# Deformable convolution on one core: tiles of 36 output bases whose samples for all nine taps come from one product, instead of patches of 128 source pixels scattered into the output

## The chip, the core and the metric

The kernel runs on one core of a Trainium2 chip. The metric is the device time of one execution in microseconds (us), from launch to the last output; the figures below are a median of three runs and one execution taken by the hardware profiler. All arithmetic is in 32-bit floats.

## The reference

The input x holds 8 images of 128 channels, 64 x 64 pixels. Two layers follow one another, each added to its own input.

Layer 0 normalises the channels in 32 groups, then does a modulated deformable convolution with 3 x 3 taps, then a batch normalisation over all images and a ReLU:

```python
om = lax.conv_general_dilated(x, off_w, (1, 1), ((1, 1), (1, 1)), ...)
off = om[:, :2 * KK].reshape(B_, KK, 2, H_, W_)
mask = jax.nn.sigmoid(om[:, 2 * KK:])
...
py = off[:, :, 0] + (row - 1.0) + ky
px = off[:, :, 1] + (column - 1.0) + kx
y0, x0 = jnp.floor(py), jnp.floor(px)
ly, lx = py - y0, px - x0
...
val = (corner(y0, x0, (1 - ly) * (1 - lx)) + corner(y0, x0 + 1, (1 - ly) * lx)
       + corner(y0 + 1, x0, ly * (1 - lx)) + corner(y0 + 1, x0 + 1, ly * lx))
val = val * mask[:, None]
out = jnp.einsum('bckhw,ock->bohw', val, w.reshape(w.shape[0], C, KK))
```

For every output pixel and each of nine taps, a learned offset (two numbers) and a mask (one) come from an ordinary 3 x 3 convolution with 27 outputs. The tap reads the image bilinearly at its shifted place, zero outside, times the mask. The nine samples are then mixed over channels by the tap's 128 x 128 weights and summed.

Layer 1 normalises in groups again and is a mixture of experts: four 3 x 3 convolutions weighted by a gate of each image, with the best two kept, and a shared one.

## The kernel before

The kernel has two ways for layer 0. `dense()` is the one that runs here: it holds for offsets under 2 in size (`REACH = 2`), which it counts as it goes; `general()` follows only where an offset is larger. The bilinear weight of a source pixel for a tap is a product of two tents, one in y and one in x: relu(1 - |distance|). For a given tap only the 5 x 5 source pixels around the tap's own place can have a weight that is not zero.

**Tables.** For each image `tables(b)` loads the image into `pad`, normalises it in place (L305-306), runs the offset convolution on TensorE (L335), writes offsets and masks to DRAM and reads them back with rows, and columns, on partitions (L351-371). Then, for each of the five distances, ScalarE computes the tents and VectorE multiplies the y tent by the mask (L386-402), and the results go to two tables in DRAM, `y_table` (SP's queue, L406) and `x_table` (POOL's queue, L416). The tables have rows of zeros at the rim. They are written one image ahead: `tables` is a generator that the main loop advances by a step here and there (`made`), so that its instructions lie between those of the loop.

**Patches.** The work is done from the side of the source. A patch is 8 rows x 16 columns of source pixels (`PR`, `PC`), the 128 of them on partitions: 256 patches for 8 images. Three steps are done for each patch and each tap row ky:

- `z_part` (L469, L475): the patch's pixels times the tap weights of three taps, a product with 384 columns; ScalarE copies it from PSUM (`pz`) to SBUF (`z`). The source pixels have been put in the patch's order before by `repack` (L240).
- `weights` (L487): VectorE multiplies the y weights (`ywts`) by the x weights (`xwts`) to get `s`: for each source pixel, three taps and each of up to 12 x 20 outputs around the patch, the bilinear weight.
- `s_part` (L508): for each tap a product of `z` (source pixel by output channel) with `s` (source pixel by output place), added in PSUM into `py`, shifted by the tap's place. Products of 18 taps, of two patches one above the other, are summed there.

`collect` (L525) then adds `py` to the half image `y` on VectorE. `end_half` takes the statistics for the batch normalisation and stores `y` to DRAM (`yd`, L546-547).

The weights of a source pixel stand at a place in the partition's row that depends on its own place in the patch, so the tables are loaded in strips: `load_tx` (POOL's queue, L437) copies one source column's x weights to the 8 partitions of that column, 16 DMAs for a block of four patches; `load_ty` (SP's queue, L451) copies one source row's y weights to 16 partitions, 8 DMAs for two patches. Places outside the strips hold zeros for good (L222).

Each engine works through its instructions in the program's order (`manual_schedule`). In the main loop the weights of the next patch come ahead of the sampling of this one:

```python
for ky in range(3):
    weights(i + 1, ky)
    s_part(i, ky, py)
    z_part(i + 1, ky)
    next(made, None)
```

A DMA waits in its queue, SP's or POOL's, until what it reads is written and the buffer that it fills is free, and those behind it wait with it.

**Layer 1** (from L820 on) reads `yd` back, applies batch normalisation and ReLU, adds the input, and does the mixture of experts as one mixed 3 x 3 convolution (L1050) for each image.

Of the kernel before, what the change touches and what calls it, by code (L numbers as in the profile page):

```python
# [16 lines left out]
P = 128  # L17
# [22 lines left out]

REACH = 2
NR = 2 * REACH + 1
PR, PC = 8, 16
NRB, NCB = H // PR, W // PC
WR, WC = PR + 2 * REACH, PC + 2 * REACH
UR, UC = WR + 2, WC + 2
ROWPAD = REACH + 1
NQI = H + 2 * ROWPAD
GSTEP = TAPS * WC
GROW = NR * GSTEP  # L50
CARRY = 24
LATER = 4
HROWS = H // 2 + 2 * ROWPAD
HSTEP = TAPS * HROWS
# [4 lines left out]
def deform_moe_conv(  # L59
# [46 lines left out]
    ystats = const.tile([P, B * NCH, 6], F32, name="ystats")  # L106
# [37 lines left out]
    def padded(pool, name):  # L144
# [9 lines left out]


    n_y, n_x = NCB * NQI * GROW, 2 * NQI * NR * HSTEP
    fill = -(-max(n_y, n_x) // (P * 256))
    tables_of = [[dram.tile([P * fill * 256], F32, name=f"tab{a}{i}") for i in range(2)] for a in "yx"]
    y_table = [
        tables_of[0][b % 2][:n_y].rearrange("(c q n) -> c q n", c=NCB, q=NQI) for b in range(B)  # L160
    ]
    x_table = [
        tables_of[1][b % 2][:n_x].rearrange("(h q n) -> h q n", h=2, q=NQI) for b in range(B)
    ]
# [11 lines left out]
    def row_range(r, ky):  # L176
        return max(0, 1 + ky - PR * r), min(WR, H - PR * r + 1 + ky)

    def col_range(c, kx):
        return max(0, 1 + kx - PC * c), min(WC, W - PC * c + 1 + kx)  # L180

    def windows(t, ky):

        one = t[:, 3 * ky : 3 * ky + 1, 2 : 2 + WC]
        return bass.AP(
            tensor=one.tensor, offset=one.offset,
            ap=[list(one.ap[0]), [PC, NCB], [WP6 - 1, 3], [1, WC]],
        )

    def dense():  # L190

        with ExitStack() as st:
# [4 lines left out]
            ap4 = st.enter_context(tc.tile_pool(name="d4", bufs=5))  # L197
            ps_c = st.enter_context(tc.tile_pool(name="ps_c", bufs=2, space=PSUM))
            ps_z = st.enter_context(tc.tile_pool(name="ps_z", bufs=3, space=PSUM))
            ps_y = st.enter_context(tc.tile_pool(name="ps_y", bufs=2, space=PSUM))  # L200

            zeros = a1.tile([P, 256], F32, name="zeros")
# [14 lines left out]


            x_wts = [a1.tile([P, WC, 3, 3, HROWS], F32, name=f"xwts{i}") for i in range(2)]
            y_wts = [a1.tile([P, 2, WR, TAPS, WC], F32, name=f"ywts{i}") for i in range(3)]  # L220
            for t in (x_wts[0], y_wts[0], y_wts[1], x_wts[1], y_wts[2]):
                nc.gpsimd.memset(t, 0.0)  # L222
# [6 lines left out]
            dw_sb = a1.tile([P, TAPS * P], F32, name="dw_sb")  # L229
            xh, ys, ss, zs = {}, {}, {}, {}  # L230
            blocks = [(b, h, c) for b in range(B) for h in range(2) for c in range(NCB)]
            patches = [(t, r) for t in range(len(blocks)) for r in range(NRB // 2)]
            per_image = len(patches) // B

            def repack(b, h):

                xh[b, h] = a2.tile([P, NRB // 2, NCB, PC, PR], F32, name="xh")
                for r in range(NRB // 2):
                    r0 = 1 + PR * (h * NRB // 2 + r)
                    nc.scalar.copy(  # L240
                        xh[b, h][:, r].rearrange("p c x y -> p y c x"),
                        pad[:, r0 : r0 + PR].rearrange("p y (c x) -> p y c x", c=NCB),
                    )
                    yield

            def tables(b):
# [8 lines left out]
                if b:  # L255
                    yield from repack(b - 1, 1)
                if b == B:
                    return
                for q in range(4):
# [5 lines left out]
                    yield  # L265
                if b < 2:
                    for t in tables_of:
                        nc.sync.dma_start(
                            out=t[b].rearrange("(p a n) -> p a n", p=P, n=256),
                            in_=zeros.unsqueeze(1).to_broadcast([P, fill, 256]),  # L270
                        )
# [842 lines left out]
```

## Time and profile before

| | |
|---|---|
| time, median of 3 runs | 2019.41 us (2015.37 to 2022.78) |
| the profiled execution's own time | 2019.38 us |
| its span | 2017.7 us |
| first sampling product (L508) | 100.7 us |
| last sampling product ends | 1631.2 us |
| layer 1 starts to load (L866) | 1640.3 us |
| TensorE busy, of the span | 1860.5 us, 92% |
| VectorE busy | 1647.3 us, 82% |
| ScalarE busy | 724.4 us, 36% |
| GpSimd (POOL) busy | 698.9 us, 35% |
| moved by DMA | 290.28 MB, mean 144 GB/s |
| mean granted clock of TensorE | 0.973 |

The profile gives, for each group of instructions, source line, engine, operation, the tiles written and read, the shapes, the count, then the busy time in us and the mean of one in ns, then the idle time of the engine just ahead of them and what ended it. PE is TensorE's matmuls, PEld its loads of weights, DVE VectorE, ACT ScalarE, POOL GpSimd; SPq is the queue of SyncE. A window gives the busy time of each engine in a stretch of the span. Every 32-bit matmul appears as two records. Times are of one execution, so durations are read from one and the same run.

### The profile page before, as it was taken

Reading aid. Unit: us, or ns where it says so; the run is one execution under the profiler, and the core shown is the slowest. Engines: PE = TensorE matmul, PEld = TensorE weight load, DVE = VectorE, ACT = ScalarE, POOL = GpSimd, SP = SyncE. Lnnn points to the kernel's source line nnn. Section 1 sums busy time; section 2 is a strip of 40 time slices with the busy share of each in tenths; the row PEclk is TensorE's granted clock in tenths of the full one; section 3 lists DMA queues with packets and bytes.
Section 4 is the critical chain, followed back from the end, with each engine's and each line's share of the span. In section 5 each row is a group of like instructions: output and inputs, shape, how many; then the busy total and the mean of one; then the engine's idle time right before and its main releaser. Section 6 shows DMA issues by size and latency. Waiting matters only on the chain. (4 is left out here: it accounts for less than half of the span.)

```text
span 2017.7 us, 25073 instructions
## 1 busy us (share of the span) xinstructions
PE 1860.5 (92%) x8146; PEld 1304.4 (65%) x8146; DVE 1647.3 (82%) x1760; ACT 724.4 (36%) x1266; POOL 698.9 (35%) x1225
## 2 busy tenths in 40 slices
PE   4099999999999999999999999999999937999999
PEld 1086787678767876786677667767888833444443
DVE  1196899599969996997799779969999959888883
ACT  1332443244324432443353234334433223333420
POOL 5323453243334342443153325333443323232220
PEclk9599999999999999999999999999999978999999
DMA  3584776477648764785478557856776554443311
GB/s 100 112 209 88 167 165 169 88 176 158 167 93 183 185 140 96 171 199 122 116 161 196 106 122 162 195 109 141 158 159 145 109 190 168 181 173 136 136 42 63
DMA packets 187755, 290.28 MB, mean 144 GB/s; under 512 B 113792, under 2 KB 119168, under 8 KB 187616
## 3 DMA queue, kind: packets, MB, share of 16 engines
q1 hardware_dynamic: 151008, 225.44, 43.6%
q0 software_dynamic: 36608, 63.14, 14.6%
q8 instruction: 68, 1.11, 0.3%
q14 instruction: 71, 0.58, 0.1%
HBM read 231.54 MB, written 56.84 MB: 143 GB/s over the span
## 5 line engine op out<-in xcount | busy, mean ns | idle before, releaser
L487 DVE TENSOR_TENSOR s<-xwts,ywts 128x684 f32<-128x684 f32 (+6 forms) x768 | 1159.4, 1564 | 80.4 <-DMA xwts<-tabx 49.8
L508 PEld LDWEIGHTS py<-s,z 128*128 128x128 f32 x4608 | 836.7, 190 | 304.4 <-issue 89.1
L508 PE MATMUL py<-s,z 128*128 128x240 f32 (+10 forms) x4608 | 993.1, 352 | 40.8 <-DVE s L487 27.2
L437 POOL DMA_DIRECT2D xwts<-tabx x1024 | 512.4, 505 | 744.1 <-DVE s L487 531.7
L475 ACT COPY z<-pz 128x384 f32<-128x384 f32 x768 | 368.8, 481 | 937.2 <-PE pz L469 936.5
L469 PE MATMUL pz<-dw_sb,xh 128*128 128x384 f32 x1536 | 624.1, 488 | 28.5 <-ACT xh L240 28.5
L469 PEld LDWEIGHTS pz<-dw_sb,xh 128*128 128x128 f32 x1536 | 285.5, 191 | 38.8 <-ACT xh L240 29.4
L1050 PE MATMUL pc<-v,u 128*128 128x512 f32 x384 | 172.5, 599 | 13.2 <-DVE v L1000 13.2
L1050 PE MATMUL pc<-v,wmix 128*128 128x512 f32 x384 | 173.5, 597 | 0.0
L897 POOL TENSOR_TENSOR x<-x,xt 128x512 f32<-128x512 f32 x64 | 90.8, 1446 | 162.8 <-ACT x L896 158.4
L335 PE MATMUL pc<-pad,offw_sb 128*32 128x504 f32 (+1 forms) x1152 | 135.1, 593 | 7.9 <-ACT pad L306 7.9
L1050 PEld LDWEIGHTS pc<-v,u 128*128 128x128 f32 x384 | 72.6, 191 | 102.8 <-issue 86.6
L1050 PEld LDWEIGHTS pc<-v,wmix 128*128 128x128 f32 x384 | 71.3, 189 | 87.0 <-issue 84.1
L525 DVE TENSOR_TENSOR y<-py,y 128x418 f32<-128x418 f32 (+2 forms) x128 | 75.7, 592 | 62.0 <-PE py L508 61.9
L416 POOL DMA_DIRECT2D tabx<-work x80 | 52.0, 653 | 205.1 <-ACT work L390 193.9
L335 PEld LDWEIGHTS pc<-pad,offw_sb 128*32 128x32 f32 x1152 | 33.4, 109 | 94.0 <-issue 81.5
L1026 ACT ACTIVATE t<-pc,bmix 128x512 f32<-128x512 f32 x32 | 22.0, 687 | 186.5 <-PE pc L1050 104.8
L318 DVE TENSOR_SCALAR om<-pc,offb_sb 128x512 f32<-128x512 f32 x16 | 12.0, 751 | 80.0 <-ACT om L315 80.0
L399 DVE TENSOR_TENSOR work<-work,mask 64x240 f32<-64x240 f32 x120 | 41.6, 403 | 36.2 <-ACT work L388 36.2
L240 ACT COPY xh<-pad 128x512 f32<-128x512 f32 x64 | 71.0, 1141 | 0.2
L930 ACT ACTIVATE pad<-x,shift,scale 128x512 f32<-128x512 f32 x64 | 47.5, 805 | 47.8 <-DVE shift L923 35.3
L896 ACT ACTIVATE x<-x,yshift,yscale 128x512 f32<-128x512 f32 x64 | 46.9, 803 | 19.9 <-DMA x<-yd 19.9
(109 smaller groups left out, 705.3 us busy)
## 6 DMA issues: line engine op xcount, KB each, us to landing
ywts<-taby SPq DMA_DIRECT2D x1024, 112.5 KB
xwts<-tabx POOLq DMA_DIRECT2D x1024, 53.4 KB, 5.8
pad<-in_x_dram SPq DMA_DIRECT2D x32, 512.0 KB
yd<-y SPq DMA_DIRECT2D x64, 256.0 KB
x<-yd SPq DMA_DIRECT2D x32, 512.0 KB
xt<-in_x_dram SPq DMA_DIRECT2D x32, 512.0 KB
out_dram<-yo SPq DMA_DIRECT2D x32, 512.0 KB
taby<-work SPq DMA_DIRECT2D x120, 60.0 KB
```

What stands on the lines that cost most here:

```text
L240: nc.scalar.copy(xh[b, h][:, r].rearrange("p c x y -> p y c x"), pad[:, r0 : r0 + PR].rearrange("p y (c x) -> p y c x", c=NCB),)
L335: nc.tensor.matmul(pc[32 * j : 32 * j + 32].rearrange("p (h w) -> p h w", w=W)[:, :, lo:hi], lhsT=offw_sb[:, k, :], rhs=pad[:, r : r + 8, ...
L416: nc.gpsimd.dma_start(out=bass.AP(tensor=x_table[b].tensor, offset=x_table[b].offset + first, ap=[[NR * HSTEP, W], [NR * HSTEP + 3 * HROWS ...
L437: nc.gpsimd.dma_start(out=flat[qx * PR : (qx + 1) * PR, qx * HSTEP : (qx + NR) * HSTEP], in_=src.unsqueeze(0).to_broadcast([PR, NR * HSTEP]),)
L469: nc.tensor.matmul(pz, lhsT=xh[b, h][:, r, c].rearrange("p x y -> p (x y)"), rhs=dw_sb[:, 3 * ky * P : 3 * (ky + 1) * P], start=True, stop ...
L475: nc.scalar.copy(zs[i][:, 3 * ky * P : 3 * (ky + 1) * P], pz)
L487: nc.vector.tensor_tensor(s[:, :, lo:hi, cl:ch], x_wts[t % 2][:, cl:ch, :, ky, first + lo : first + hi].rearrange("p c k r -> p k r c"), y ...
L508: nc.tensor.matmul(py[:, top + lo : top + hi, cl - kx + 2 : ch - kx + 2], lhsT=zs[i][:, k * P : (k + 1) * P], rhs=s[:, kx, lo:hi, cl:ch], ...
L525: nc.vector.tensor_tensor(part, py[:, rl:rh, cl:ch], part, ALU.add)
L897: nc.gpsimd.tensor_tensor(y, y, xt[:, c * CH : (c + 1) * CH], ALU.add)
L930: nc.scalar.activation(pad2[:, 1 + 8 * c : 9 + 8 * c, 1 : W + 1], x1[:, c * CH : (c + 1) * CH].rearrange("p (h w) -> p h w", w=W), AF.Iden ...
L1050: nc.tensor.matmul(pc, lhsT=us[j][:, kx], rhs=vs[g][:, rows, kx : kx + W], start=(kx == 0), stop=(kx == 2),)
```

## The change

Layer 0's `dense()` is turned round: the work is done from the side of the output, and the tap weights come last.

- **Tiles and bands.** The output has 66 x 66 bases with its rim, cut in 11 x 11 tiles of 6 x 6 = 36 (`T`). A base stands for the place to which a tap at its own offset 0 points, so the sample of tap (ky, kx) at output (r, c) belongs to base (r + ky, c + kx). The samples of a tile need 10 x 10 = 100 source pixels (`Q`, `QQ`). A band is one row of 11 tiles; there are 88 bands and 968 tiles.
- **Source pixels on partitions.** After normalising, `tables` transposes the image on TensorE (32 transposes of 128 x 128), ScalarE copies them out of PSUM, and two DMAs for each group of four write them to `pixels` in DRAM, pixel by pixel with 128 channels. Ten DMAs from DRAM to DRAM rearrange these as `tiled`, so that one DMA for each band (`xts`) brings, for every tile, its 100 pixels onto 100 partitions.
- **Weights.** One VectorE product for each tile makes `s`: for each of 100 source pixels the weights of all nine taps at 36 bases, 324 elements. The y and x weights come by 10 DMAs each for every band (`load`), on SP's and POOL's queues, with 10 equal copies each; three buffers of each.
- **Sampling.** One product for each tile (`sample`), 100 x 128 by 100 x 324, gives all taps' samples in channel order; ScalarE copies them to `samples`, a strip of 8 rows x 66 columns for each tap. Its first two rows are copied from the band before.
- **Tap weights.** Nine products for each band (`conv`), 128 x 128 by up to 384 columns, sum the taps in PSUM, one band behind the sampling. `finish` adds the bias on ScalarE, takes the statistics and stores.
- **Out go** `z_part`, `s_part`, `collect`, `start_half`, `end_half`, `repack`, `load_tx`, `load_ty`. The table writes change in form: y weights with 3 DMAs for each distance in runs of 66 elements, x weights with 3 in runs of 18. The advance of `tables` in the loop is 14 steps a band. The offset convolution, the tents and layer 1 stay as they are; `bn_aggr` moves from layer 1's head to the end of layer 0.

The diff, cut to its core:

```diff
-PR, PC = 8, 16
...
+T = 6
+Q = T + 2 * REACH
+QQ = Q * Q
+NT1 = (H + 2) // T
+WB = W + 2
...
+    pixels = dram.tile([H, NQI, P], F32, name="pixels")
+    tiled_of = [dram.tile([NQI, Q, NT1, P], F32, name=f"tiled{i}") for i in range(2)]
...
-            x_wts = [a1.tile([P, WC, 3, 3, HROWS], F32, name=f"xwts{i}") for i in range(2)]
-            y_wts = [a1.tile([P, 2, WR, TAPS, WC], F32, name=f"ywts{i}") for i in range(3)]
...
+            x_wts = [a1.tile([P, NT1, T, TAPS, T], F32, name=f"xwts{i}") for i in range(3)]
+            y_wts = [a1.tile([P, T, TAPS, WB], F32, name=f"ywts{i}") for i in range(3)]
...
+            samples = [a1.tile([P, TAPS, T + 2, WB], F32, name=f"samples{i}") for i in range(2)]
...
+                def store_pixels(g, px):
+                    xtb = a2.tile([P, 4, P], F32, name="xtb")
+                    nc.scalar.copy(xtb, px)
+                    for odd in range(2):
+                        nc.sync.dma_start(
+                            out=pixels[8 * g + odd : 8 * g + 8 : 2, ROWPAD : ROWPAD + W].rearrange(
+                                "t w c -> w t c"
+                            ),
+                            in_=xtb[64 * odd : 64 * odd + 64],
+                        )
+
                 for c in range(NCH):
                     nc.scalar.activation(part[c], part[c], AF.Identity, bias=shift, scale=scale)
-                    if c % 2:
-                        yield
+                    yield
+                    px = ps_c.tile([P, 4, P], F32, name="px", tag="pc")
+                    for t in range(4):
+                        nc.tensor.transpose(px[:, t], part[c][:, t * P : (t + 1) * P], ident)
+                    behind.append((c, px))
+                    if c:
+                        store_pixels(*behind.pop(0))
+                    yield
+                store_pixels(*behind.pop(0))
...
+                    if c == 0:
+                        for qx in range(Q):
+                            nc.sync.dma_start(
+                                out=tiled[ROWPAD : ROWPAD + H, qx],
+                                in_=bass.AP(
+                                    tensor=pixels.tensor,
+                                    offset=pixels.offset + qx * P,
+                                    ap=[[NQI * P, H], [T * P, NT1], [1, P]],
+                                ),
+                            )
+                            if qx % 2:
+                                yield
...
+            def load(g, q):
...
+                b, j = bands[g]
+                lo, hi = max(0, q - 2 * REACH), min(T, q + 1)
+                r = lo - q + 2 * REACH
+                nc.sync.dma_start(
+                    out=y_wts[g % 3][q:QQ:Q, lo:hi].rearrange("p a b c -> p (a b c)"),
+                    in_=bass.AP(
+                        tensor=y_table[b].tensor,
+                        offset=y_table[b].offset + (T * j + q) * GROW + r * YSTEP,
+                        ap=[[0, Q], [1, (hi - lo) * YSTEP]],
+                    ),
+                )
+                nc.gpsimd.dma_start(
+                    out=x_wts[g % 3][q * Q : (q + 1) * Q, :, lo:hi].rearrange(
+                        "p t a b c -> p t (a b c)"
+                    ),
+                    in_=bass.AP(
+                        tensor=x_table[b].tensor,
+                        offset=x_table[b].offset + q * HROW + (j * NR + r) * XSTEP,
+                        ap=[[0, Q], [T * HROW, NT1], [1, (hi - lo) * XSTEP]],
+                    ),
+                )
+                if q == 0:
+                    xts[g] = a3.tile([P, NT1, P], F32, name="xt")
+                    tiled = tiled_of[b % 2]
+                    nc.sync.dma_start(
+                        out=xts[g][0:QQ].rearrange("p t c -> p (t c)"),
+                        in_=tiled[T * j : T * j + Q].rearrange("q x t c -> x q (t c)"),
+                    )
...
+                s = a6.tile([P, TAPS, T, T], F32, name="s")
+                nc.vector.tensor_tensor(
+                    s[0:QQ],
+                    x_wts[g % 3][0:QQ, c].rearrange("p a k r -> p k r a"),
+                    y_wts[g % 3][0:QQ, :, :, T * c : T * c + T].rearrange("p r k a -> p k r a"),
+                    ALU.mult,
+                )
...
+            def sample(n):
+                g, c = divmod(n, NT1)
+                pq = ps_q.tile([P, TAPS, T, T], F32, name="pq")
                 nc.tensor.matmul(
...
+                    lhsT=xts[g][0:QQ, c],
+                    rhs=ss.pop(n)[0:QQ].rearrange("p k r a -> p (k r a)"),
                     start=True, stop=True,
                 )
...
+                nc.scalar.copy(samples[g % 2][:, :, 2 : T + 2, T * c : T * c + T], pq)
+
+            def conv(g, n, py):
...
+                nc.tensor.matmul(
+                    py[:, first:],
+                    lhsT=dw_sb[:, 3 * ky + kx],
+                    rhs=samples[g % 2][:, n, first + ky : T + ky, kx : kx + W],
+                    start=(n == 0), stop=(n == TAPS - 1),
+                )
...
+            for g in range(len(bands) + 1):
...
+                if j:
+                    nc.scalar.copy(samples[g % 2][:, :, 0:2], samples[(g - 1) % 2][:, :, T : T + 2])
+                for c in range(NT1):
+                    if g < len(bands):
+                        n = g * NT1 + c
+                        weights(n + AHEAD)
+                        sample(n)
+                        if c < Q:
+                            load(g + 2, c)
+                    if g and c > 1:
+                        conv(g - 1, c - 2, py)
+                    next(ended, None)
                     next(made, None)
-                    if ky == 0 and i % 2:
+                    if c % 3 == 2:
                         next(made, None)
```

## The prediction

> **What bounds the kernel now.** I read the page first: busy times, then the slices.
>
> ```profile
> PE 1860.5 (92%) x8146; PEld 1304.4 (65%) x8146; DVE 1647.3 (82%) x1760; ACT 724.4 (36%) x1266; POOL 698.9 (35%) x1225
> ...
> PE   4099999999999999999999999999999937999999
> ...
> DMA  3584776477648764785478557856776554443311
> ```
>
> TensorE (PE) is full from 100 us on, with one dip at 1640 us, where the second layer begins. Next, the windows query: one window over the whole sampling loop, two in the start-up, one where the second layer loads.
>
> ```profile
> 100.70:1632.00 1531.30, 1496.01 (x7174) 1144.94 (x7174) 1333.70 (x1187) 579.45 (x1057) 557.33 (x1077) 1.00 0.65 147
> ```
> ```profile
> 86.00:92.00 6.00, 0.00 (x0) 0.00 (x0) 0.00 (x0) 0.00 (x0) 2.04 (x5) 0.50 0.82 131
> 92.00:99.00 7.00, 0.00 (x0) 0.00 (x0) 0.00 (x0) 0.00 (x0) 2.95 (x6) 0.50 0.68 139
> ```
> ```profile
> 1650.00:1700.00 50.00, 26.22 (x63) 12.49 (x64) 38.13 (x75) 17.62 (x26) 22.90 (x16) 0.71 0.69 267
> ```
>
> After window and length come PE, PEld, DVE, ACT, POOL busy, then granted clock, DMA share, GB/s. In the loop PE is busy 98% at full clock: it sets the pace, VectorE (DVE) follows at 87%. Second reading: from 86 to 99 us every engine waits for the tables' loads alone, and these deliver only 131 and 139 GB/s; long rows (1650 to 1700) run at 267.
>
> The chain that ended last gives PE's rate, the groups by shape DVE's, the groups the rest.
>
> ```profile
> 1951.16 62.16 PE pc L1050 x144
> ```
> ```profile
> L487 DVE TENSOR_TENSOR s<-xwts,ywts 128x720 f32<-128x720 f32 x288 | 462.6, 1658 | 4.3 <-DMA ywts<-taby 4.3
> ...
> L487 DVE TENSOR_TENSOR s<-xwts,ywts 128x513 f32<-128x513 f32 x32 | 39.3, 1227 | 0.0
> ```
> ```profile
> L508 PE MATMUL py<-s,z 128*128 128x240 f32 (+10 forms) x4608 | 993.1, 352 | 40.8 <-DVE s L487 27.2
> L437 POOL DMA_DIRECT2D xwts<-tabx x1024 | 512.4, 505 | 744.1 <-DVE s L487 531.7
> L475 ACT COPY z<-pz 128x384 f32<-128x384 f32 x768 | 368.8, 481 | 937.2 <-PE pz L469 936.5
> L469 PE MATMUL pz<-dw_sb,xh 128*128 128x384 f32 x1536 | 624.1, 488 | 28.5 <-ACT xh L240 28.5
> ...
> L240 ACT COPY xh<-pad 128x512 f32<-128x512 f32 x64 | 71.0, 1141 | 0.2
> ```
>
> Each matmul is recorded twice: 144 records are 72 matmuls of 512 columns in 62.16 us, so a column costs 62.16/(72x512) = 1.686 ns.
>
> The profiled execution, 2019.38 us (the median of the three is 2019.41), is: 100.7 to the first sampling matmul, 1530.5 of loop, 9.1 to the second layer's first load at 1640.3, 377.4 of second layer, 1.7 around the span. The change touches the first three.
>
> **PE: removed and added.** Out go 768 products of 384 columns (z) and 2304 of, by the shapes, 503,424 columns (s): 798,336 x 1.686 = 1346 us. In come 968 products of 324 columns and nine convolution taps for each of 88 bands (384 columns, 256 in each image's first): 313,632 + 294,912 columns = 1026 us. The offset convolution stays, seven images in the loop at 16.5 us (144 records in the window 300 to 500): 115. New are 224 transposes of 128 columns: between 128 columns' 0.216 us and two weight loads of 190 ns, 0.38; I take 0.38, since every transpose loads new weights: 85 us (48 at least). Sum 1226. Today the loop takes 1530.5 against 1346 + 115 = 1461, 4.7% more; with the same supplement 1284 us. PE saves 246 us.
>
> **DVE.** From the shapes 513 and 720 a product costs 160 ns + 2.08 ns an element. The new one has 324 elements and still reads xwts with a wide step: 834 ns, 968 times: 807 us. Bounds: 1.05 ns an element, as L399's 403 ns for 240, makes 500 ns (484 us); runs of six elements may push it to 1100 ns (1065 us, an estimate one third above the row). With 50 us of statistics and seven images of tables at about 14 us: 955 us (630 to 1215). Below PE even at the top. collect (75.7 us) goes.
>
> **ScalarE (ACT).** The z copies go (369 us), xh too (71). 968 copies of 324 elements come, written in runs of six: between 431 ns, scaled from L475, and 722, scaled from L240's strided 1141; I take 500: 484 us (417 to 699). Two-row copies between bands: 88 of 1188 elements, 1.2 to 2.6 us, take 1.9: 167. Output 88 x 0.6 = 53, pixel copies 56 x 0.69 = 39, tables 7 x 21 = 147. Sum 890, at most 1165: beside PE. At a band's edge ACT waits for the last tap, then does output and two-row copy, about 2.5 us, before it frees a pq; three buffers and the free first two taps cover most. PE loses perhaps 0.3 us a band, 26 us, within the supplement.
>
> **Queues.** SP: 188 DMAs an image instead of 166; at 0.45 to 0.9 us about 105 us of the 161 that PE needs for an image. The tiled copies wait there for the pixel stores and hold up the loads behind them; those are two bands (29 us) ahead. POOL issues ten x loads a band and 15 table writes an image at 0.5 to 1.1 us, 75 us an image: covered.
>
> **DMA.** Loop bytes now: table loads 118 + 56 MB. Then: y rows 88 x 713 KB = 62.7 MB, x rows the same, source tiles 88 x 563 KB = 49.6 MB, outputs 16.8, and seven images of 10.3 MB (input 2.1, pixels 2.1, tiled 3.6, tables 1.5, offsets 1.0) = 72. Together 264 MB instead of about 225 in a shorter loop. The 125.4 MB of tables are broadcasts. At the start-up window's 139 GB/s they take 902 us, the other 138.6 MB at 267 GB/s 519: 1421 us, above PE. From the other side: the same kinds of load beside others ran at 198 GB/s between 110 and 115 us:
>
> ```profile
> 110.00:115.00 5.00, 5.00 (x24) 4.19 (x23) 4.26 (x5) 2.33 (x4) 0.00 (x0) 1.00 0.90 198
> ```
>
> That makes 633 + 519 = 1152. The mean, 1287, equals PE's 1284. I take it, since the new loads have longer y runs than now but shorter x runs (216 to 1080 B for 6840). Two resources equally full delay each other where the table work crowds into the first seven of eleven bands; I add 45 us (0.5 a band, my estimate): loop 1330.
>
> A rule to weigh against these rows: the Trainium skill, "DMA: Bandwidth & Descriptors", section "Why a DMA increments its semaphore by 16 and not by 1", says that a transfer runs on the largest number of engines up to 16 that divides the slowest dimension of both sides, 10 for 100 partitions, the lowest ten on SP's queue. All y and tile loads would then sit on ten engines: 11.2 MB each, with 9.5 MB of the rest, at 267/0.69/16 = 24 GB/s 860 us; by the rule alone the sum would be that of PE alone, 1781, by the rows 1827. No row of this trace shows engines apart.
>
> **Start and end.** Start-up: smaller memsets free POOL 4.5 us earlier (22.8 to about 18.3), transposes and pixel copies put 7 us ahead of the offset convolution, the tiled DMAs delay offsets some 3, tents and table writes add 4, the first band's 2 MB land about 4 sooner: +6 (0 to 15), first product at 107. Band 0 has no convolution and runs at DVE's pace: +3. End: one band's taps are already counted, statistics are shorter: 8 for 9.1.
>
> Sum: 107 + 3 + 1330 + 8 + 377.4 + 1.7 = **1827 us**.
>
> **Rivals.**
> - DMA hides wholly and PE sets the loop, 1284: 107 + 3 + 1284 + 8 + 379 = 1781; with the cheap transposes 1743. For it: PE is 98% busy now. Against: 264 MB in 1284 us is 206 GB/s, and no 100 us of today's loop exceeds 186. Chance 0.25.
> - DMA sets the loop at the start-up's rate: 1421 + 497 = 1918 (1880 to 2009). POOL already waits 174.9 us for its own earlier loads:
>
> ```profile
> POOL xwts L437 <- DMA xwts<-tabx: 174.9, 273, 4.4
> ...
> SPq L451 <- DMA ywts<-taby: 56.9, 52, 3.5
> ```
>
>  Chance 0.15.
> - Slower: broadcasts to ten partitions deliver less than today's to sixteen and eight. Scaled by 10/16, 139 becomes 87 GB/s; midway, 113, they take 1110 us, with 519 the loop is 1629, the time 2126. It decides below 125 GB/s (125.4 MB in 1522 - 519 us), only 10% under the measured 139. Against it: y loads for 16 copies and x loads for 8 mix at that rate, so ten is no outlier. Chance 0.18, with 0.04 more about the crossing.
> - ACT or DVE as the bound: needs both tops at once and still stays at 1215; 0.03, near 1800.
>
> **How the numbers follow.** Forecast, balanced PE and DMA, 1785 to 1880: 0.35. Faster: 0.35 + 0.25 + 0.15 + 0.03 = 0.78; within 0.5% (about what a measurement of this kernel can tell from no change) 0.04; slower 0.18. The range 1735 to 2060 leaves out a tenth at the top, nearly as much below.
>
> **What would show it.** Right: PE's 1936 sample and 1584 tap records at 1.686 ns a column; the product near 834 ns; loop GB/s near 200; DVE's waits for xwts and ywts landings short, a few us at most, mostly in the table bands. Wrong: PE under 85% of the loop with DVE waiting for loads (the DMA rivals), gaps that pull the granted clock below 1.00, or a product beyond 1.1 us.

## The result and the profile after

The changed kernel takes 2122.6 us (median of four, 2120.4 to 2137.6) against 2018.9 for the kernel before on the same chip: 1.053 times as long, 95% interval 1.048 to 1.058. The forecast was 1827 us, faster. The profiled execution took 2120.77 us with a span of 2118.9.

The page of the changed kernel: busy times, then three rows of the slices.

```profile
PE 1703.3 (80%) x5778; PEld 906.1 (43%) x5778; DVE 1101.9 (52%) x1768; ACT 846.6 (40%) x1658; POOL 745.0 (35%) x1124
...
PE   4048877888788879796988698869899965999999
...
PEclk9568998998899889988999899989999986999999
DMA  6887687868786878687778777877877726344311
```

PE's row of nines is broken: it is 80% busy, and no other engine is busier. The transfer engines are busy 0.6 to 0.8 all through the loop, never full for the length of a slice. The bytes were forecast rightly (264.8 MB between the first and the last product, 264 forecast), their rate was not: 165 GB/s, where near 200 was named as the sign of being right. The loop runs from the first product (114.1 us) to the last tap (1729.9): 1616 us where 1333, with the first band's 3, was forecast. Of the miss of 295 us all but some 11 is in the loop.

The windows query over one image (the third), in three pieces, and over the last image, which makes no tables any more. After window and length: PE, PEld, DVE, ACT, POOL busy, granted clock, DMA share, GB/s.

```profile
538.20:578.40 40.20, 25.52 (x72) 15.81 (x73) 21.51 (x38) 9.87 (x22) 8.06 (x14) 0.75 0.75 181
578.40:683.30 104.90, 90.50 (x382) 44.39 (x380) 46.77 (x67) 51.52 (x105) 34.54 (x55) 0.93 0.72 165
683.30:748.20 64.90, 54.31 (x166) 32.96 (x165) 32.44 (x51) 28.51 (x61) 35.81 (x58) 0.89 0.84 153
```
```profile
1579.00:1717.00 138.00, 130.43 (x427) 81.83 (x426) 86.71 (x131) 65.82 (x138) 51.23 (x86) 0.96 0.71 154
```

Bands are cut here at the first DVE product of each; DVE runs up to three tiles ahead of PE. Bands 0 and 1 take 40 us, where two bands of the last image take 25; there the next image is loaded into `pad`. Bands 2 to 6 hold the transposes, the offset convolution and the trip of offsets and masks through DRAM. Bands 6 and 7 hold the table writes, and bands 7 to 10 otherwise only sampling and loads. An image with tables takes 209 us, the last one 138.

The groups by line, the new ones that the forecast priced:

```profile
L497 PE MATMUL pq<-s,xt 100*128 100x324 f32 x1936 | 758.4, 485 | 285.1 <-DVE s L486 163.0
L486 DVE TENSOR_TENSOR s<-xwts,ywts 100x324 f32<-100x324 f32 x968 | 676.9, 754 | 462.5 <-DMA xwts<-tabx 167.1
...
L503 ACT COPY samples<-pq 128x324 f32<-128x324 f32 x968 | 412.5, 439 | 818.3 <-PE pq L497 814.8
L510 PE MATMUL py<-samples,dw_sb 128*128 128x384 f32 (+1 forms) x1584 | 659.8, 500 | 0.0
```

The product takes 754 ns (834 forecast), the copy 439 (500): the parts are cheaper than priced. And the waits, as engine, line, what it waited for, total, times, longest:

```profile
POOL xwts L462 <- DMA xwts<-tabx: 217.2, 161, 5.3
DVE s L486 <- DMA xwts<-tabx: 167.1, 21, 29.2
...
DVE s L486 <- DMA ywts<-taby: 95.7, 27, 11.6
```

The longest, 29.2 us, is the start-up's. Without it DVE stands 234 us in the loop for windows that have not landed, PE behind it; before it was 44 (49.8 and 18.5, less 24.3 in the start-up).

### The profile page after: what moved, and what is told of

It reads as the page before. It is cut to its first block, busy times and chain, and to the rows that moved or that the text cites. A ratio compares the mean times of both kernels' runs of the same rounds, so it can differ in the third digit from the quotient of the medians.

```text
span 2118.9 us, 20665 instructions
## 1 busy us (share of the span) xinstructions
PE 1703.3 (80%) x5778; PEld 906.1 (43%) x5778; DVE 1101.9 (52%) x1768; ACT 846.6 (40%) x1658; POOL 745.0 (35%) x1124
## 2 busy tenths in 40 slices
DMA packets 265454, 335.21 MB, mean 158 GB/s; under 512 B 106716, under 2 KB 211956, under 8 KB 261812
## 5 line engine op out<-in xcount | busy, mean ns | idle before, releaser
L497 PE MATMUL pq<-s,xt 100*128 100x324 f32 x1936 | 758.4, 485 | 285.1 <-DVE s L486 163.0
L486 DVE TENSOR_TENSOR s<-xwts,ywts 100x324 f32<-100x324 f32 x968 | 676.9, 754 | 462.5 <-DMA xwts<-tabx 167.1
L503 ACT COPY samples<-pq 128x324 f32<-128x324 f32 x968 | 412.5, 439 | 818.3 <-PE pq L497 814.8
L510 PE MATMUL py<-samples,dw_sb 128*128 128x384 f32 (+1 forms) x1584 | 659.8, 500 | 0.0
L497 PEld LDWEIGHTS pq<-s,xt 100*128 100x128 f32 x1936 | 371.5, 206 | 626.4 <-issue 269.3
L510 PEld LDWEIGHTS py<-samples,dw_sb 128*128 128x128 f32 x1584 | 320.6, 202 | 151.2 <-issue 28.8
L437 POOL DMA_DIRECT2D tabx<-work x120 | 93.7, 847 | 219.4 <-ACT work L417 201.4
L524 DVE BATCH_NORM_STATS2 ystats<-y 128x6 f32<-128x384 f32 (+1 forms) x88 | 47.9, 545 | 139.6 <-ACT y L521 139.4
L316 PE MATMUL px<-ident,pad 128*128 128x128 f32 x256 | 46.0, 309 | 61.2 <-ACT pad L312 61.1
L550 ACT COPY samples<-samples 128x1188 f32<-128x1188 f32 x80 | 94.0, 1175 | 0.0
```

The lines of the kernel that those rows point to most:

```text
L316: nc.tensor.transpose(px[:, t], part[c][:, t * P : (t + 1) * P], ident)
L437: nc.gpsimd.dma_start(out=bass.AP(tensor=x_table[b].tensor, offset=x_table[b].offset + (k + i) * HROW + r * XSTEP + 3 * k * T, ap=[[HROW, ...
L486: nc.vector.tensor_tensor(s[0:QQ], x_wts[g % 3][0:QQ, c].rearrange("p a k r -> p k r a"), y_wts[g % 3][0:QQ, :, :, T * c : T * c + T].rear ...
L497: nc.tensor.matmul(pq.rearrange("p k r a -> p (k r a)"), lhsT=xts[g][0:QQ, c], rhs=ss.pop(n)[0:QQ].rearrange("p k r a -> p (k r a)"), star ...
L503: nc.scalar.copy(samples[g % 2][:, :, 2 : T + 2, T * c : T * c + T], pq)
L510: nc.tensor.matmul(py[:, first:], lhsT=dw_sb[:, 3 * ky + kx], rhs=samples[g % 2][:, n, first + ky : T + ky, kx : kx + W], start=(n == 0), ...
```

## The experiments

Eighteen kernels ran, each beside the kernel before (2016 to 2022 us). The theories stand in the expectations: TEN (ten transfer engines are the limit), BROADCAST and BANK (the reads get in each other's way), PORT (the limit is on the side of the writes or in the engines), CHAIN (in-order waits of the table stage), RATE (only the bytes count), FIFO (the order in SP's queue), STRETCH (each stretch of bands has its own bound). None but STRETCH came through, and that not in every number. Kernels that leave out loads, tables or copies serve only to find what these cost.

**Ten engines: row order, xt split, y loads on POOL.** The edits (the first is a control for the second):

```diff
-  out=y_wts[g % 3][q:QQ:Q, lo:hi]...   out=x_wts[g % 3][q * Q : (q + 1) * Q, :, lo:hi]
+  out=y_wts[g % 3][q * Q : (q + 1) * Q, lo:hi]...   out=x_wts[g % 3][q:QQ:Q, :, lo:hi]
-  nc.sync.dma_start(out=xts[g][0:QQ]..., in_=tiled[...].rearrange("q x t c -> x q (t c)"))
+  for a, z in XT_PARTS:   # ((0, 100),), then ((0, 96), (96, 100))
+      nc.sync.dma_start(out=flat[a:z], in_=rows[a:z])
```
```diff
-  nc.sync.dma_start(out=y_wts[g % 3]...
+  nc.gpsimd.dma_start(out=y_wts[g % 3]...
```

> Control for the three runs beside it: the 100 source pixels of a tile stand on the partitions as row*10+column instead of column*10+row, so that the ten copies of a y row land on neighbouring partitions and those of an x row on every tenth one; xt then comes with its rows in order. No byte, no packet size and no number of transfers changes. Every theory expects the changed kernel's 2122 us again, within 15 us; a larger move would say that the place of the partitions decides.

> As the control, with the load of xt cut in two (96 and 4 partitions). Theory TEN (the loads of y and of xt sit on ten of the sixteen DMA engines and those ten are what the loop waits for): per band the ten engines carry 0.713 MB of y and 0.563 MB of xt at about 140 GB/s (9.1 us) and their share of 0.713 MB of x (3.2 us), 12.3 us beside bands that took 13 where only loads ran. With xt on sixteen this is 5.1 + 5.7 = 10.8 us or less, so 1.5 to 2 us a band less in the stretches that go by transfers, 100 to 170 us in all: 1950 to 2020 us. Theory BROADCAST (ten copies of the same DRAM rows read at half rate whatever engine does it): within 25 us of 2122. Theory CHAIN (the in-order waits of the table stage set the time, transfers merely take long): within 30 us of 2122.

> The changed kernel with its y loads issued by POOL beside the x loads; nothing else moves. Theory TEN: if POOL's queue spreads ten packets over changing engines, as the x loads show, the ten engines lose 0.713 MB of y: 4.0 us for xt and 6.4 us for y and x on sixteen, 10.4 us a band instead of 12.3, 120 to 190 us less: 1930 to 2000 us; POOL issues 20 transfers a band at 0.6 to 0.7 us, 13 us a band, and could itself become the wait, which caps the gain. Theory BROADCAST: within 25 us of 2122. Theory CHAIN: within 40 us of 2122, with SP's queue shorter by ten issues a band.

> Control order, xt cut into 96 and 4 partitions and y loads issued by POOL: none of the three large loads is bound to ten engines. Theory TEN: 1.989 MB a band over sixteen engines at 14 GB/s each is 8.9 us, below PE's 12.5 us a band (that of the last image, which has no tables); images with tables fall from 204-214 us to 165-180: 1830 to 1920 us, so below the kernel before (2019). Theory BROADCAST: 2090 to 2140 us, packets as long as before. Theory CHAIN: 2050 to 2130 us.

Measured: 2113.3 (row order), 2113.1 (with xt split), 2310.0 (y on POOL), 2266.8 (both). The split does nothing beyond its control. The queue lines of the page, of the control and of the split one (packets, MB, share of 16 engines):

```profile
q1 hardware_dynamic: 216436, 264.68, 50.3%
```
```profile
q1 hardware_dynamic: 217316, 264.69, 53.4%
```

The same bytes occupy the engines longer with the split. Counting the trace's packets in flight between the first and the last product of the last image shows both sides. In the control they are exactly ten for 32% of the time, and one to nine for about 3%; with the split, exactly ten for 20%. But the 5632 B packets of xt took 410 ns on average for 301, and the longest of y 1080 for 968. The count of ten fits the rule that the prediction cited from the Trainium skill ("DMA: Bandwidth & Descriptors", "Why a DMA increments its semaphore by 16 and not by 1"), as far as how many engines work; which ones they are, no row here shows. That this sets the time, TEN, is wrong.

The row order does something else. Pieces whose ten copies go to every tenth partition move faster than pieces whose copies go to ten neighbours: over the loop, by the trace's packets, x pieces went from 11.8 to 13.0 B/ns when they got the wide places, and y pieces from 15.4 to 14.1 when they lost them.

The y loads on POOL were a miss for every theory: POOL then issues twenty loads a band (1055 us of issues) and waits 288 us for its own earlier loads, and the last image, without tables, takes 173 us.

**What the parts cost: tables, y loads, x loads, and ten rows for one.** The edits:

```diff
-  made = tables(b + 1) if b + 1 < B else iter(())
+  made = tables(b + 1) if b < 1 else iter(())        # and tables of b % 2 loaded
```
```diff
+  if g < 3:                                          # around the y loads; then around the x loads
```
```diff
-  ap=[[0, Q], [1, (hi - lo) * YSTEP]]
+  ap=[[GROW, Q], [1, (hi - lo) * YSTEP]]             # x: [HROW, Q] likewise
```

> Leaves out the tables of images 3 to 8 (their transposes, stores, tiled copies, offset convolution and table writes); their bands load the rows of images 1 and 2 again, so samples, taps and loads stay. It measures what the table stage costs the loop under every theory: images 2 to 7 took 204 to 215 us with it, and the last image, which makes no tables, 138. Theory RATE (transfers move at some 165 GB/s whatever issues them; the loop ends when 264 MB are moved): a band of loads only is 2.0 MB, 12.1 us, under PE's 12.5, so images 2 to 7 take 138 to 145 us, 6 x 66 = 400 us less: 1700 to 1740 us. Theory CHAIN (in-order waits of the table stage): the same, 1700 to 1740. If the bands stay above 15 us, the loads alone pace the loop and the total is above 1800.

> Leaves out the y loads after the first three bands (the windows keep old values); all else as in the changed kernel. Theory RATE: 0.713 MB of about 2.9 MB a band are gone, 60 of 264 MB, 24% of a loop of 1615 us that goes by transfers: bounded below by PE's 1284 us, so 300 to 330 us less: 1790 to 1830 us. Theory CHAIN (waits for the table stage's small transfers and for its pieces in order): SP is free of ten issues a band, DVE of its 96 us of waits for y windows: 20 to 100 us less, 2020 to 2100.

> Leaves out the x loads after the first three bands instead. Theory RATE: the same bytes as the y loads, so the same 1790 to 1830 us; if one of the two kinds costs more (x comes as pieces of up to 4320 B, y as pieces of up to 11,880 B) the dearer one shows the shorter time. Theory CHAIN: POOL, which waits 217 us for its own earlier x loads, issues the table writes at once; DVE loses 167 us of waits for x windows: 50 to 150 us less, 1970 to 2070.

> The ten copies of every y and x row are read from ten neighbouring table rows instead of ten times from the same one (the values are then those of other rows; sizes, counts and places of the writes stay). Theory BROADCAST (reads of the same DRAM row by ten transfers at once stand in each other's way): packets shorten and the loop nears PE's pace, 1830 to 1950 us. Theory RATE, with reads no slower from one row than from ten: within 25 us of 2122. Theory CHAIN: within 25 us of 2122.

Measured: 1776.9 without tables, 1991.1 without y loads, 1903.3 without x loads, 2129.5 with ten rows. BROADCAST falls with the last. Windows over one table-free image of the kernel without tables, and over one image with tables and the last image of the kernel without x loads:

```profile
788.70:941.20 152.50, 136.73 (x433) 82.76 (x434) 86.92 (x133) 67.68 (x140) 66.19 (x112) 0.96 0.80 157
```
```profile
300.30:482.30 182.00, 163.61 (x621) 91.25 (x620) 101.20 (x155) 90.17 (x186) 12.17 (x16) 0.94 0.59 149
1372.00:1500.00 128.00, 127.99 (x438) 81.76 (x437) 88.12 (x132) 66.50 (x142) 0.00 (x0) 1.00 0.39 118
```

Three prices follow. PE alone needs 128 us an image at full clock. With all loads and no tables an image takes 151 (mean of six), 24 MB at 159 GB/s: the loads by themselves are slower than PE. With tables but without x loads the image shown takes 182, of which PE is idle 18. Neither RATE nor CHAIN gave these: taking 23% of the loop's bytes away shortened the loop by 8% or 13%, not by 20%, and x loads cost 88 us more than y loads of the same size (by the trace's packets x pieces ran at 11.8 B/ns in the changed kernel, y pieces at 15.4).

**Waits of the table stage, crowded DRAM, table writes on ACT.** The edits:

```diff
-  yield from pause(6)      # before bn_stats
+  yield from pause(20)
...
-  yield from pause(6)      # before mask's sigmoid
+  yield from pause(12)
```
```diff
-  tensor=y_table[b].tensor, ... ap=[[0, Q], [1, (hi - lo) * YSTEP]]
+  tensor=x[b].tensor, ... ap=[[12 * HW, Q], [1, (hi - lo) * YSTEP]]     # x: [[HW, Q], [10 * HW, NT1], ...]
```
```diff
-  nc.gpsimd.dma_start(out=bass.AP(tensor=x_table[b].tensor, ...
+  nc.scalar.dma_start(out=bass.AP(tensor=x_table[b].tensor, ...
```

> The table stage of an image has steps to spare before band 9; 14 more of them are left between the loads of the image into pad and the first bn_stats (20 instead of 6), and 6 more between the loads of mask and its sigmoid (12 instead of 6). Nothing else moves, and no byte. Theory CHAIN (DVE and ACT stand in order behind bn_stats, which waits for pad, and mask, which waits for its two trips through DRAM, and hold up the products and the copies behind them): the 14 us in which PE idles in the second band of each image go, and some of the 6 in the seventh, 10 to 16 us an image, seven images: 2005 to 2055 us. Theory RATE (the loop ends when its 264 MB are through at 165 GB/s): within 25 us of 2122, with the products waiting for y and x windows instead.

> The same with the pixels in row order on the partitions, which by itself gave 2113 instead of 2122 us. Every theory: 5 to 12 us below the run with the pauses alone.

> The loads of y and x windows read the image x instead of the tables: ten rows 196 KB apart for y, eleven pieces of rows 160 KB apart for x, so that the same sizes and counts come from 2 MB instead of two stretches of about 119 KB a band (values are then wrong; writes, queues and engines stay; the loads also no longer wait for table writes). Theory BANK (reads crowd in a small stretch of DRAM): pieces of 4320 and 11,880 B, which ran at 9 to 13 B/ns with 14 or more packets in flight and 26 when alone, run at 18 or more, and images 2 to 7 take 180 to 190 us, as without x loads: 1900 to 1960 us. Theory PORT (the limit is on the side of the writes into ten partitions, or in the engines): packets as long as before, within 30 us of 2122.

> The pauses, and the fifteen table writes of x an image issued by ACT, which computes the tents, instead of POOL: POOL no longer waits for ACT (201 us in all) with the x loads behind it, and ACT has 15 issues of some 0.8 us more an image, 12 us. Theory CHAIN: x windows land earlier, DVE loses part of its 167 us of waits for them, 5 to 15 us an image off the run with the pauses alone, less what ACT's issues delay the copies (0 to 8): 0 to 60 us below that run. Theory RATE: within 20 us of it, or above it, since the 880 packets of each write are the same.

Measured: 2136.0, 2077.4, 2165.1, 2259.2. BANK falls, and PORT's range (within 30 us of 2122) is missed too, on the slow side. CHAIN falls: the statistics moved and the stall in the second band stayed. From the timeline of the run with pauses (start, length, engine, line; in brackets the idle time before it and what ended it):

```profile
348.59 1.03 SPq L238 DMA_DIRECT2D pad<-in_x_dram  x2
350.89 16.52 SPq L454 DMA_DIRECT2D ywts<-taby  x8
```
```profile
373.47 0.75 DVE L486 TENSOR_TENSOR s<-xwts,ywts 100x324 f32<-100x324 f32 x1 [16.87 <-DMA ywts<-taby]
```
```profile
359.63 0.71 PE L497 MATMUL pq<-s,xt 100*128 100x324 f32 x2
...
374.32 1.42 PE L497 MATMUL pq<-s,xt 100*128 100x324 f32 x2 [13.54 <-issue]
```

DVE waits for y windows, not for `pad`; SP, whose single y issues take 0.71 and 0.72 us just before, spends 16.5 us on eight, right behind the loads into `pad`. Hence FIFO, below. Two results no theory had. Row order with pauses gained 59 us where 5 to 12 were expected. The pieces changed as in the first pair (x 12.7 B/ns for 11.2, y 13.9 for 16.1), but there the row order gained 9 us, so the other 50 stay open. And table writes from ACT cost 123 us. POOL's queue had gathered their 72 B runs into packets of up to 3168 B; on ACT's they go one by one (191,196 packets under 512 B instead of 106,716), and x loads waited 101.5 us for them instead of 59.0 in the run with pauses.

**The order in SP's queue, and the pixel copies.** The edits: the loads into `pad` two images ahead, one in each of the last four bands (alone; with row order and other pauses; the same, issued by ACT); and, from the third image on, no pixel stores and tiled copies.

```diff
-  for q in range(4): nc.sync.dma_start(out=pad[...], in_=x[b]...)      # first steps of tables(b)
+  if j >= NT1 - 4 and c == 5 and b + 2 < B:                             # in the main loop
+      image(b + 2, j - NT1 + 4)
```
```diff
-  for qx in range(Q):
+  for qx in range(Q if b < 2 else 0):
...
-  for odd in range(2):
+  for odd in range(2 if b < 2 else 0):
```

> Moves one thing: the four loads of an image into pad (0.5 MB each, on SP) leave the first steps of the image before, where they stand in SP's queue between the y loads of two bands, and go one each into the last four bands of the image two before. bn_stats stays at its step. Theory FIFO (SP's queue is served in order: in the run with pauses DVE waited 16.9 us for y windows in the second band of an image while SP spent 16.5 us on eight y loads behind pad): the 13 to 15 us of PE idle time in the second band go, of which 2 to 5 come back in the last four bands, seven images minus the first: six times 9 to 13 us, 2040 to 2070 us. Theory RATE (the bytes have to be moved somewhere): within 25 us of 2122.

> The same move with the pixels in row order, bn_stats eight steps earlier (pad has landed long before) and mask six later (pause 12). Theory FIFO: the run with pauses and row order gave 2077 us; its stall of 14 us in the second band goes too, less 2 to 5 back in the last bands: 2000 to 2030 us, level with the kernel before (2019). Theory RATE: 2065 to 2090.

> As the run before, with the four loads into pad issued by ACT, so that they aren't ahead of y loads on any queue. Theory FIFO: the 2 to 5 us an image that come back in the last bands stay away: 5 to 30 us below the run before, 1985 to 2020 us, unless ACT stands behind its own issues (four of some 0.6 us an image, 2.4 us). Theory RATE: within 15 us of the run before.

> Leaves out, from the third image on, the stores of the transposed pixels and the ten copies into the tiled layout (2.1 MB and 3.6 MB an image, in packets of 512 B; xt is then read from old tiles). Theory RATE: 5.7 of about 30 MB an image, 19% of 209 us, bounded by what PE and the chain need (181 us without x loads): 25 to 29 us an image, six images: 1950 to 1975 us. Theory FIFO: only what stands behind these transfers in SP's queue, the y loads of the third to sixth band, where PE idles 8 us an image in all: 2060 to 2110 us.

Measured: 2168.5, 2081.1, 2090.6, 2115.1. One image (the third) of the first, in the same cuts as above:

```profile
566.90:597.20 30.30, 26.64 (x73) 17.17 (x74) 21.45 (x38) 9.67 (x21) 6.46 (x11) 0.77 0.72 170
597.20:701.70 104.50, 90.17 (x381) 44.17 (x379) 46.75 (x67) 51.41 (x104) 35.29 (x56) 0.93 0.73 166
701.70:780.70 79.00, 60.06 (x170) 35.70 (x168) 32.73 (x51) 30.22 (x63) 37.01 (x60) 0.86 0.89 152
```

The first two bands fall from 40 to 30 us, as FIFO said: the stall was what it took it for. But the last four, where the bytes went, grow from 65 to 79, and the kernel became slower (2168.5) where FIFO had 2040 to 2070. With row order and pauses the move changed nothing (2081.1 beside 2077.4), and issuing from ACT was no help; FIFO missed both, and RATE, which said that bytes cost the same anywhere, holds these two. It falls with the fourth kernel: 5.7 MB an image less in bands 3 to 6 gave 7.5 us in all, though 267 GB/s, the rate of the long loads in the prediction, would have made it 21 us an image. FIFO's range ends 5 us below that one.

**The same bytes in PE's stretch.** The row order stays. A second `pad` tile lets the loads run beside the convolution; then the convolution is stretched by one idle step after each tap group.

```diff
+  if 1 <= j < 5 and c == 5 and b + 2 < B:
+      image(b + 2, j - 1)                       # into pads[b % 2]
...
-  yield                                         # after each tap group of the offset convolution
+  yield from pause(2)
```

> Same bytes as the run with early loads into pad, 2081 us, but a second pad tile, so that the four loads for the image after next go one each into the second to fifth band, where PE works on transposes and the offset convolution and the transfer engines' share was 0.60 to 0.77, instead of the last four bands, where it was 0.81 to 0.97. (To make room: four s tiles instead of six, two y tiles instead of three, zeros in a tile that is needed later.) Theory STRETCH (an image is a stretch of bands that PE paces and a stretch that transfers pace; its time is the sum of the longer one in each, so bytes cost only in the second): the last four bands, 70.6 us together, lose the 0.5 MB each at 5 us a MB and more, 10 to 14 us an image, six images, and the second to fifth band gain 0 to 4: 2005 to 2045 us. Theory RATE (bytes cost the same wherever they are moved): 2070 to 2090.

> The run before with one idle step after each of the 18 tap groups of the offset convolution, so that PE's extra work of some 18 us an image lies in four bands instead of two to three and more transfers run beside it. Theory STRETCH: bands in which PE was the bound grow fewer by what the transfer-paced ones take over, 3 to 8 us an image, 20 to 55 us below the run before, less what the later tables cost the last bands (0 to 5 us an image): 0 to 40 us below it. Theory RATE: within 12 us of it.

Measured: 2046.2 and 2016.3 us; against the kernel before 1.012 (1.009 to 1.015) and 0.998 (0.996 to 1.001). The third image of each:

```profile
534.00:561.60 27.60, 21.69 (x83) 13.86 (x84) 21.92 (x39) 13.30 (x27) 9.99 (x17) 1.00 0.75 180
561.60:665.90 104.30, 88.52 (x368) 44.71 (x367) 47.27 (x67) 47.60 (x100) 33.10 (x53) 0.93 0.86 182
665.90:728.00 62.10, 53.83 (x172) 32.68 (x170) 33.43 (x51) 28.43 (x61) 33.99 (x56) 0.95 0.82 165
```
```profile
521.00:550.30 29.30, 24.09 (x86) 14.86 (x85) 22.07 (x38) 13.71 (x28) 10.57 (x17) 0.94 0.75 177
550.30:643.70 93.40, 87.38 (x371) 43.85 (x370) 45.56 (x64) 39.53 (x80) 30.17 (x50) 0.96 0.84 198
643.70:712.80 69.10, 56.59 (x164) 33.43 (x163) 36.28 (x54) 37.35 (x79) 38.13 (x60) 0.88 0.84 157
```

The run to compare with is the early load in row order (2081.1). By the means below, the last four bands lose 6.5 us an image with the second tile, and the middle stretch, which takes the 2 MB over, gains 1.7; the image shown has a DMA share of 0.86 there. Stretching the convolution takes 11 us from the middle and gives 6 back at the end, where the tables now come later. STRETCH missed the first run by 1 us at its edge, with less in the last bands than the 10 to 14 us an image that it had said, and held the second; RATE, which had no gain in either, missed both. Both kernels also have four s tiles for six and two y tiles for three, which was not tried apart, and some 11 of the 35 us between 2081.1 and 2046.2 lie in the first image, whose loads moved too. Means of images 3 to 6, between the first DVE products of the bands:

| kernel | bands 0-1 | 2-6 | 7-10 | image | last image | us |
|---|---|---|---|---|---|---|
| changed | 40.3 | 103.3 | 65.7 | 209.3 | 137.9 | 2122.6 |
| no tables | 27.9 | 67.8 | 55.5 | 151.1 | 139.7 | 1776.9 |
| no x loads | 28.8 | 99.5 | 50.7 | 179.0 | 128.4 | 1903.3 |
| no pixel copies | 39.4 | 99.5 | 67.8 | 206.7 | 140.7 | 2115.1 |
| pad early only | 29.9 | 104.7 | 78.7 | 213.3 | 147.4 | 2168.5 |
| pad early, row order | 29.7 | 103.2 | 70.2 | 203.1 | 129.7 | 2081.1 |
| second pad tile | 29.5 | 104.9 | 63.7 | 198.1 | 128.2 | 2046.2 |
| convolution stretched | 29.7 | 93.5 | 69.5 | 192.6 | 126.3 | 2016.3 |

The sums by image hold, within a us, wherever one cuts. The first two columns do not: cut at PE's first products, the last three rows have 42, 40 and 38 in bands 0 and 1 and 93, 97 and 86 in bands 2 to 6, since PE starts on the transposes before its first product of band 2.

The last version beats the changed kernel by 5% and is level with the kernel before.

## Why the prediction was wrong

**What held.** The bytes, and PE's term: 1284 us forecast; without x loads PE is busy 1266 us from the first product to the last tap. In the changed kernel, at a lower clock, it is 1335. DVE's and ACT's terms were a little high, both stayed beside PE. Start, tail and second layer held: first product at 114 for 107. Two of the prediction's own signs of being wrong came: PE under 85% of the loop (1335 of 1616 is 83%) with DVE waiting for loads, and a clock below 1.00.

**The step that failed** is the loop's: "The mean, 1287, equals PE's 1284 ... I add 45 us". It has two faults.

The price of the broadcasts was taken midway between two rows, 139 and 198 GB/s, and that made the loads of a band 1.43 MB at 163 and 0.76 at 267, 11.6 us, just under PE's 12.2. Without tables a band takes 13.7. An image is then 24.0 MB in 150.7 us; if its 8.3 MB of xt and output went at 267 GB/s, an estimate, the 15.7 MB of broadcasts ran at 131. The start-up window, where nothing but such loads ran, was the right row (it gives 13.1 us a band); the window at 198 lasted 5 us. At 139 the transfers alone make 1421, as the prediction itself had it.

And the table stage was to cost only PE's part, 28.6 us an image (30 with the supplement); its transfers were to vanish beside it, but for the 45 us. Band by band, in us, means of images 3 to 6:

| band | 0 | 1 | 2 | 3 | 4 | 5 | 6 | 7 | 8 | 9 | 10 |
|---|---|---|---|---|---|---|---|---|---|---|---|
| changed | 13.4 | 26.9 | 14.1 | 28.7 | 27.5 | 9.1 | 23.9 | 19.2 | 18.4 | 14.6 | 13.5 |
| no tables | 14.1 | 13.8 | 14.0 | 13.3 | 14.2 | 12.8 | 13.5 | 14.2 | 13.3 | 14.4 | 13.6 |

The stage costs 58 us an image. Some 25 lie in bands 3 to 5, where PE has its extra work: that is PE's term, and it was priced well. The other 33 stood in the sum only as the 45 us, 6 an image:

- 13 in band 1: y loads behind the loads into `pad` in SP's queue. "Those are two bands (29 us) ahead" was said to cover it; it did not, since SP takes 16.5 us for eight issues when its earlier loads are slow. With nothing but those loads moved ("pad early only"), band 1 took 16.5.
- 10 in band 6, the trip of offsets and masks through DRAM (ACT waited 64.1 us in eight waits for mask), with PE idle 6.6 us. Without x loads band 6 is as long. That it is the trip was not tried apart.
- 10 in bands 7 and 8. The table writes fit by place and size, but were not left out alone: their packets (264 B at 7.6 B/ns, up to 3168 B at 7.7) run in bands 6 and 7 and took the time of all sixteen engines for 12 us an image, where 1.5 MB at 267 GB/s had been put at 5.6.

So the miss comes out of two runs: the loads alone make 151 us an image for PE's 134, eight times 17; the stage makes 58 for 30, seven times 28, less the 45 allowed: 136 + 196 - 45 = 287, and the loop was 286 above its 1330. Eight times 151.1 and seven times 58.2 are 1616, as measured.

That work in one stretch can't use the slack of another, the windows being only two bands ahead, is what the last two experiments speak for, with the reservations made there: nearly the same bytes and the same products took 203 us an image, then 198 and 193, as the loads into `pad` and the convolution were laid beside each other.

PE's side of the same loop: without x loads it is 1400 us, 1266 of PE and 134 idle; x loads bring 219 (2122.6 less 1903.3). Of these, 69 are PE's own time at a lower clock, 1335 for 1266.

**The slower rival** gave 2126 us, 3 us off, and its mechanism was wrong: broadcasts at 113 GB/s and a loop as long as one sum of transfers. They ran at about 131, above the 125 at which that rival itself decided; taking 5.7 MB an image away changed 7.5 us, and moving 2 MB without removing a byte changed 35 (with the tile counts changed too). A rival that hits the number has not been shown by it.

**Ten engines** in the cited rule: the count of ten in flight fits, but freeing xt of them did not help, since the packets lengthened. What caps such loads near 160 GB/s stays open: not the same row, not a small stretch of DRAM, not the number of engines by itself. The place of the partitions written has a part in it, as the row order shows; how much, and what the engines' own handling of packets adds, was not tried.

## What to carry to other kernels

Price a kind of load by the window in which it ran alone and saturated, not by a mean with a short mixed one: here that row gives 13.1 us a band, 13.7 were measured and 11.6 were taken. Before two resources' totals are compared, cut the loop into stretches as long as the buffers can look ahead; a transfer is free only in a stretch that something else paces, and where loads already set the pace, added work shows in full. If a change frees the bound engine, ask first what in the old loop had its slack from that engine: here the new loop only reached the old time when the loads into `pad` and the offset convolution were moved so that they overlap.

## What the runs showed of the hardware

A gap costs PE twice. After 13.54 us without work the next pair of sample products took 1.42 us instead of 0.71 (lines above); the trace's record has half clock there from 364.29 to 384.77 us. The clock records of the changed kernel show half clock 37 times in the loop, for 324 us together, idle time included, in whole multiples of 3.4 us; the kernel before had three such steps in its loop. The Trainium skill ("TensorE: Matmul & The Clock Gate", "Part 1: The HAM clock gate") says that an idle window of 3.4 us halves the clock and a busy one restores it; the steps agree.

A packet of these loads slows with the number in flight. In the changed kernel the few that ran almost alone went at 26 B/ns (7128 B in 271 ns, 11,880 B in 446); with fourteen or more in flight on average these two took 539 and 974 ns, and 4320 B took 393, 11 to 13 B/ns. The loops of the changed kernel and of the versions that move the same bytes from the same queues ran at 160 to 178 GB/s.
